# Merging the map chains of two batches, and queueing mixing earlier, in a gated cross-attention and stream-mixing kernel

## The chip, the cores and the metric

The kernel runs on one core of a Trainium2 chip. The metric is the device time of one execution in microseconds. The kernel before takes 1831.41 us (median of 3 runs, 1829.26 to 1835.13). The execution that the profiler recorded took 1828.05 us, of which its span, from the first recorded instruction to the last, is 1825.9 us.

The engines are named as in the profile: PE (TensorE, matmul), PEld (its weight loads), DVE (VectorE), ACT (ScalarE), POOL (GpSimd) and SP (SyncE, which issues every transfer here). Each runs its own list of instructions in order, and they wait for each other through semaphores.

## The reference

The input x has 8 batches of 512 rows and 2048 columns. There are two residual stages, each on a layer-normed x.

```python
x = x + tanh(g_xattn) * xattn(layernorm(x), ctx, mask, Wq..bo)
x = x + tanh(g_ffn)   * ffn(layernorm(x), W_res, W_pre, W_post, ...)

# ffn: every row is a token of 4 streams of 512
x_norm = x * rsqrt(mean(x*x) + eps)
H_res  = sinkhorn(x_norm @ W_res.T + base, 50 iterations, tau=0.1)   # 4x4
H_pre, H_post = softmax(x_norm @ W_pre.T + ..), softmax(x_norm @ W_post.T + ..)
H_res  = (1-g)*I + g*H_res
y      = (sum_n H_pre[n] * x[n]) @ W_branch
out[i] = sum_j H_res[i,j] * x[j] + H_post[i] * y
```

The first stage cuts the 2048 columns into patches of 128 and runs attention with 8 heads inside each patch. The second stage needs a whole row of the first stage's result before it can begin: the layer norm and the 24 logits of a token are sums over all 2048 columns. From the logits it makes the token's maps (a 4 x 4 matrix by Sinkhorn's iteration, and two softmaxes of 4), and then mixes the four streams with them.

## The kernel before, in words

**The main loop.** A batch has 16 patches, so there are 128 patches in order, counted by t. For each t the function `act` emits the pieces of work that the letters of ORDER name: scores and their maxima (`smax`, three patches ahead), exponentials (`expo`), attention times values (`attv`), output projection (`outp`), the projections of a later block of four patches (`proj`, `stack`, `vproj`), statistics of a later batch (`stats`), and steps of mixing (`mixstep`). The result x1 of the first stage goes to DRAM (x1s).

**The chain of maps.** When the last block of a batch has been projected (`outp` of block n-1, at t = 16(b+1) + 3), `rawmap` gathers the batch's sums and `ffn` emits its maps. A batch has 512 tokens, which lie as 4 groups on 128 partitions, so a 4 x 4 matrix per token makes tiles of 128 x 64 (E, L, W) and 128 x 16 (sm, uv). After a prologue of norms, logits and softmaxes come 49 sweeps of six DVE instructions each, L844 to L854: multiply, row sum, reciprocal, multiply, column sum, reciprocal. Each needs the result of the one before it. Every ten sweeps the scale factors are folded back with a logarithm and an exponential on ACT (L858, L840). L873 writes the finished map Et. This dependent series is called the chain of that batch.

CHAINS says which batches form one chain. `ffn` takes a list of batches and makes its tiles 4 groups wide for each; NTM, the width for which tiles are reserved, is four times the longest entry of CHAINS. A chain is emitted when its last batch is complete.

**Mixing.** There are two forms. `mixv` (L909 to L951) works on 128 tokens, called a chunk, mostly on DVE: it loads four streams, makes the weighted sum xpre with ACT and POOL, runs the branch matmul, and makes each of the four outputs with L939 (ACT), L943/L944 (ACT, POOL), L946 and L949 (DVE). The main loop takes its steps from a queue, mixq: an entry may begin at t + LAGS[b], where t is the patch at which the chain was emitted, and then 3.25 steps are taken per patch. A chunk has 13 steps.

`mixp` (L953 to L1005) works on a chunk mostly on PE. Its first half loads the rows (xc), makes xpp with four matmuls (L967), transposes it (L974) and runs the branch matmuls (L905 to L907, with plb made on DVE at L902). Its second half multiplies with two matrices QD and HD (L1000, L1001), which POOL builds (L988, L990). HD is built from HR, which is the batch's Et written to DRAM (L885) and read back in another layout (L887). PD, for the first half, is built from rec, which takes the same way (L796, L798) but is ready early in the chain. PE_MIX says which chunks are mixed in this way: chunk 3 of batch 4, all of batches 5 and 6, and chunks 1 to 3 of batch 7. They are kept in tailq and run after the last patch, in this order. They are written (4,3), (5,0) and so on below. The last pieces are those of batch 7's remaining chunk, a `mixv`.

**The order on each engine** isn't written by hand. A scheduler places the instructions of each engine by readiness in its own timing model and by priority, and the engine then runs the list in that order. The pieces have priority 0, and the chain has -1000, so a chain instruction that is ready goes first. A tile pool with n buffers makes the n-plus-first user wait for the first one's readers.

The lines that the change touches:

```python
LAGS = (30,) * 8                                                      # L53
CHAINS = ((0,), (1,), (2,), (3,), (4,), (5,), (6,), (7,))             # L81
PE_MIX = ((), (), (), (), (3,), (0, 1, 2, 3), (0, 1, 2, 3), (1, 2, 3))# L79
NTM = 4 * max(len(c) for c in CHAINS)                                 # L713
for grp in CHAINS:                                                    # L1112
    if grp[-1] == bb_ - B + 8:
        ...
        res = at("chain", ffn, grp)
        for q, maps in zip(grp, res):
            mixq.append((t + LAGS[bb_], mix(q, maps)))
            for c_ in PE_MIX[q - B]:
                tailq.append(mixp(q, c_, maps))
```

Of the kernel before, what the change touches and what calls it, by code (L numbers as in the profile page):

```python
# [49 lines left out]
PRI = dict(load=0, smax=0, expo=0, attv=0, outp=0, proj=0, stack=0, vproj=0, stats=0, mix=0, chain=-1000, raw=0)  # L50
EARLY = 4
LATE = 3000
LAGS = (30,) * 8  # L53
NV = 2
MIXN = 2
MIXP = (3.25,)*4
# [21 lines left out]
BUF_XP = 16  # L78
PE_MIX = ((), (), (), (), (3,), (0, 1, 2, 3), (0, 1, 2, 3), (1, 2, 3))  # L79
SPLITS = (1, 1, 1, 1, 1, 1, 1, 1)  # L80
CHAINS = ((0,), (1,), (2,), (3,), (4,), (5,), (6,), (7,))  # L81
BUF_SK = 2
PE_IN = ((), (), (), (), (), (), (), ())
HDP = 'xtp'
# [15 lines left out]
def gated_xattn_mhc_kernel(  # L100
# [611 lines left out]

    NTM = 4 * max(len(c) for c in CHAINS)  # L713

# [176 lines left out]
    def mix(b, maps):  # L891
        E, cst, pre, prc, post, rec, HR = maps
        for c in range(4):
            if c in PE_IN[b - B]:
                yield from mixp(b, c, maps, True)
            elif c not in PE_MIX[b - B]:
                yield from mixv(b, c, maps)
# [149 lines left out]
    def act(c, t):  # L1047
# [54 lines left out]
        elif c == "O":  # L1102
# [3 lines left out]
            if n >= 1 and p == 3:  # L1106
                at("outp", run, og_[0])
                bb_, kk_ = divmod(n - 1, NBLK)
                if kk_ == NBLK - 1:
                    at("raw", rawmap, bb_)  # L1110
                    p0 = tc.cur_priority
                    for grp in CHAINS:  # L1112
                        if grp[-1] == bb_ - B + 8:
                            grp = [q + B - 8 for q in grp if q + B - 8 >= 0]
# [4 lines that stand above are left out]
# [77 lines left out]
```

## Time and profile before

| | |
|---|---|
| median of 3 runs | 1831.41 us (1829.26 to 1835.13) |
| profiled execution | 1828.05 us, span 1825.9 us |
| granted PE clock, mean | 0.932 |
| PE busy | 1547.1 us, 85% |
| DVE busy | 1382.3 us, 76% |
| ACT busy | 1069.4 us, 59% |
| POOL busy | 602.8 us, 33% |
| 49 sweeps of 8 chains on DVE (L844 to L854, records added up) | 606.8 us in 2312 instructions |
| the chain of batch 0, first copy to Et | about 300 to 508 us |
| of batch 5 | about 1320 to 1610 us |
| of batch 6 | about 1515 to 1703 us |
| of batch 7 | 1642 to 1769 us |
| exponential of the last patch (L597) | between 1610 and 1620 us; the tail then runs to 1826 us |

How to read the rows below. A row of busy time by stage gives the stretch, its length, then the busy time of PE, PEld, DVE, ACT and POOL with the number of instructions, the granted clock of PE (1.00 is full), the share of the DMA engines and GB/s. If it is asked for one source line, it has only the engine of that line. A row of the time order gives start, duration, engine, line, operation, output and inputs, shape, and in brackets how long the engine had been idle before it and what ended that. Records of neighbouring DVE instructions can overlap: what an instruction costs its neighbours is the distance between starts.

### The profile page before, as it was taken

The numbers are of one execution on the slowest core, as the hardware profiler recorded it, in microseconds if no ns is written. First come the engines' busy times: TensorE is split into PE (matmuls) and PEld (weight loads), VectorE is DVE, ScalarE is ACT, GpSimd is POOL, SyncE is SP. The second block draws the span as 40 slices with busy tenths as digits, with TensorE's granted clock in tenths as the row PEclk, the third lists the DMA queues.
The fourth block names the chain that finished last, engine by engine and source line by source line (L and its number), as shares of the span: only waits on it lengthen the run. The fifth ranks groups of instructions, "written<-read, shape, count | busy, mean of one in ns | idle before, by whom it ended". The sixth has DMA issues, their size and how long they took to land.

```text
span 1825.9 us, 32268 instructions
## 1 busy us (share of the span) xinstructions
PE 1547.1 (85%) x10517; PEld 901.0 (49%) x10517; DVE 1382.3 (76%) x4201; ACT 1069.4 (59%) x2030; POOL 602.8 (33%) x511
## 2 busy tenths in 40 slices
PE   3998999989889888889878888799888889768887
PEld 2554555555555554545544445455455555543333
DVE  7434345877888778888888879889898998998761
ACT  2386466646555656558565475566665566755454
POOL 0512222322232243342444333444334442321121
PEclk7999999999999988999988999899999999989999
DMA  6478696467646855568555784468755565523443
GB/s 214 139 209 256 208 258 194 140 174 232 180 134 200 254 169 165 151 192 269 162 154 164 214 251 144 139 196 259 215 154 165 148 189 147 172 93 119 144 157 117
DMA packets 353237, 330.60 MB, mean 181 GB/s; under 512 B 53351, under 2 KB 251303, under 8 KB 353070
## 3 DMA queue, kind: packets, MB, share of 16 engines
q1 hardware_dynamic: 353070, 328.55, 60.6%
q8 instruction: 83, 1.36, 0.3%
q14 instruction: 84, 0.69, 0.1%
HBM read 226.71 MB, written 101.16 MB: 180 GB/s over the span
## 4 chain that ended last, share of the span: by engine, by line
PE 37%; DVE 23%; DMA 18%; issue 9%; ACT 9%; POOL 4%; SPq 1%; ACTq 0%; POOLq 0%; DVEq 0%
PE vp L559 5%; DVE w L946 4%; DMA xs<-in_x_dram 4%; PE qk L518 3%; PE qk L519 3%; DMA out_dram<-w 3%; PE qk L520 3%; DMA x<-x1s 2%; PE mx L1000 2%; DMA x1s<-xt 2%; PE lgx L448 2%; DVE mx L571 2%; PE op L667 2%; DVE W L844 2%; PE mx L1001 2%
## 5 line engine op out<-in xcount | busy, mean ns | idle before, releaser
L559 PE MATMUL vp<-Wv,ct 128*128 128x256 f32 x1024 | 272.4, 418 | 16.7 <-DMA ct<-in_cx_dram 15.1
L500 POOL TENSOR_SCALAR xn<-xt,ln_r,nb 128x512 f32<-128x512 f32 x128 | 105.5, 826 | 501.2 <-DMA xt<-in_x_dram 385.7
L559 PEld LDWEIGHTS vp<-Wv,ct 128*128 128x128 f32 x1024 | 207.4, 210 | 68.0 <-issue 18.6
L518 PE MATMUL qk<-xh,WqkH 128*128 128x512 f16 x512 | 199.2, 390 | 29.4 <-ACT xh L505 16.3
L946 DVE SCALAR_TENSOR_TENSOR w<-x,Et,w 128x512 f32<-128x512 f32 x180 | 180.0, 1001 | 49.6 <-POOL w L944 34.0
L519 PE MATMUL qk<-xl,WqkH 128*128 128x512 f16 x512 | 197.9, 387 | 4.3 <-POOL xl L507 4.0
L520 PE MATMUL qk<-xh,WqkL 128*128 128x512 f16 x512 | 197.6, 386 | 0.0
L571 DVE TENSOR_REDUCE mx<-smax 128x8 f32<-128x1024 f32 x128 | 154.9, 1210 | 41.7 <-PE smax L569 41.3
L507 POOL TENSOR_TENSOR xl<-xn,xh 128x512 f16<-128x512 f32 x128 | 156.3, 1228 | 76.0 <-ACT xh L505 70.4
L597 ACT ACTIVATE e<-sT,ebi,esc 128x1024 f32<-128x1024 f32 x128 | 153.4, 1198 | 18.0 <-PE sT L595 17.9
L523 DVE SCALAR_TENSOR_TENSOR ev<-qk,bqs,ev 128x512 f16<-128x512 f32 x128 | 94.5, 739 | 77.5 <-ACT ev L522 76.1
L667 PE MATMUL op<-gh,WoH 128*128 128x512 f32 x256 | 120.9, 474 | 35.3 <-DVE ev L523 31.1
L944 POOL TENSOR_TENSOR w<-w,pj 128x512 f32<-128x512 f32 x60 | 80.1, 1334 | 213.1 <-ACT w L939 113.7
L505 ACT CAST xh<-xn 128x512 f16<-128x512 f32 x128 | 78.3, 612 | 103.7 <-POOL xn L500 102.9
L522 ACT ACTIVATE ev<-qk,bqs 128x512 f16<-128x512 f32 x128 | 86.9, 679 | 85.0 <-PE qk L520 78.7
L673 ACT ACTIVATE junk<-xt,nmean 128x512 bf16<-128x512 f32 x128 | 91.6, 716 | 73.9 <-DVE xt L671 41.3
L850 DVE TENSOR_TENSOR W<-E,uv 128x64 f32<-128x64 f32 x392 | 119.4, 307 | 5.4
L844 DVE TENSOR_TENSOR W<-E,uv 128x64 f32<-128x64 f32 x352 | 117.1, 335 | 4.8
L612 PE MATMUL u<-e,onesb 128*32 128x256 f32 x1024 | 102.7, 403 | 10.5 <-DVE mq L573 3.8
L668 PE MATMUL op<-gl,WoH 128*128 128x512 f32 x256 | 107.1, 418 | 0.0
L669 PE MATMUL op<-gh,WoL 128*128 128x512 f32 x256 | 106.6, 417 | 0.0
L632 POOL TENSOR_TENSOR o<-o,mb 128x1024 f32<-128x1024 f32 x32 | 75.6, 2364 | 93.2 <-ACT o L627 85.9
(287 smaller groups left out, 3504.6 us busy)
## 6 DMA issues: line engine op xcount, KB each, us to landing
xt<-in_x_dram SPq DMA_DIRECT2D x128, 256.0 KB
ct<-in_cx_dram SPq DMA_DIRECT2D x128, 256.0 KB
xTt<-in_xT_dram SPq DMA_DIRECT2D x128, 256.0 KB
qd<-ev SPq DMA_DIRECT2D x128, 256.0 KB
x1s<-xt SPq DMA_DIRECT2D x128, 256.0 KB
xs<-in_x_dram SPq DMA_DIRECT2D x112, 256.0 KB
QS<-qd SPq DMA_DIRECT2D x192, 128.0 KB
KS<-qd SPq DMA_DIRECT2D x192, 128.0 KB
```

The source lines that it names most:

```text
L507: G.tensor_tensor(l, xn, h, ALU.subtract)
L518: T.matmul(ps, WqkH[:, c, ms], hs[c], start=(c == 0), stop=False)
L519: T.matmul(ps, WqkH[:, c, ms], ls[c], start=False, stop=False)
L520: T.matmul(ps, WqkL[:, c, ms], hs[c], start=False, stop=(c == 3))
L559: T.matmul(ps[:, h, :], ct[:, c, :], Wv[:, c, :], start=(c == 0), stop=(c == 3))
L571: V.tensor_reduce(mx, sc, AX.X, ALU.max)
L597: A.activation(e32, sc, AF.Exp, bias=ebi[:, t : t + 1], scale=esc[:, t : t + 1])
L667: T.matmul(ps, WoH[:, e, cs], gh[:, e], start=(e == 0), stop=False)
L668: T.matmul(ps, WoH[:, e, cs], gl[:, e], start=False, stop=False)
L844: V.tensor_tensor(W4[:, h], E4[:, h], vb[:, h], ALU.mult)
L850: V.tensor_tensor(W4[:, h], E4[:, h], ub[:, h], ALU.mult)
L946: V.scalar_tensor_tensor(w, x1[j], E[:, n, 4 * j + i : 4 * j + i + 1], w, ALU.mult, ALU.add)
```

## The change

Two constants change. Batches 1 and 2 share a chain, as do 3 and 4, and 5 and 6; batches 0 and 7 keep their own. A chain of two batches is emitted at the patch at which its second batch was emitted before (t = 51, 83 and 115), and its tiles are 8 groups wide: 128 x 128 for E, L and W, 128 x 32 for sm and uv. As NTM is now 8, the tiles of batches 0 and 7 are the first half of such tiles. LAGS is looked up by the batch that completes the chain, so every entry but batch 0's is now 18. Both batches of a pair are queued for mixing at the same patch: 69 for batches 1 and 2 (65 and 81 before), and 101 for batches 3 and 4 (97 and 113 before). The order of tailq is the same.

```diff
-LAGS = (30,) * 8
+LAGS = (30, 18, 18, 18, 18, 18, 18, 18)
-CHAINS = ((0,), (1,), (2,), (3,), (4,), (5,), (6,), (7,))
+CHAINS = ((0,), (1, 2), (3, 4), (5, 6), (7,))
```

## The prediction

> **What bounds the kernel now.** I read the page's busy shares first, then busy time by stage, then the time order of DVE, PE and POOL after the last patch. The stages are cut where a batch's chain begins (its first copy, L710 and L724), so each but the last is the time of 16 patches.
>
> ```profile
> span 1825.9 us, 32268 instructions
> PE 1547.1 (85%) x10517; PEld 901.0 (49%) x10517; DVE 1382.3 (76%) x4201; ACT 1069.4 (59%) x2030; POOL 602.8 (33%) x511
> ...
> 297.00:471.00 174.00, 157.21 (x1174) 96.18 (x1168) 129.19 (x407) 103.44 (x208) 51.82 (x46) 0.96 0.63 183
> 883.00:1105.00 222.00, 183.00 (x1283) 109.14 (x1282) 184.76 (x554) 132.78 (x259) 86.41 (x69) 0.92 0.64 188
> 1323.00:1514.00 191.00, 165.60 (x1191) 102.12 (x1190) 175.03 (x502) 117.04 (x214) 84.11 (x68) 0.93 0.57 167
> 1642.00:1826.00 184.00, 156.86 (x484) 56.47 (x482) 114.56 (x530) 89.38 (x157) 28.71 (x32) 0.99 0.40 136
> ```
>
> The columns are PE, PEld, DVE, ACT, POOL, granted clock, DMA. Sixteen patches with one chain and no mixing take 174 us (10.9 a patch); with mixing 222 and, once the statistics are done, 191. TensorE is the busiest engine throughout, at 90% without mixing and 82% with it, and DVE comes close (92% in the third row). So DVE relief can pay there, but only where PE waits for it. The last 184 us have no attention left: PE works through the PE chunks.
>
> ```profile
> 1645.72 1.12 PE L1000 MATMUL mx<-ys,QD 128*128 128x512 f32 x2 [0.68 <-ACT ys L985]
> 1660.43 0.38 PE L907 MATMUL yp<-WbH,plb 128*128 128x512 f16 x1
> 1661.48 1.12 PE L1000 MATMUL mx<-ys,QD 128*128 128x512 f32 x2 [0.68 <-ACT ys L985]
> 1675.92 1.10 PE L1000 MATMUL mx<-ys,QD 128*128 128x512 f32 x2 [0.77 <-ACT ys L985]
> ...
> 1703.14 0.25 DVE L873 TENSOR_TENSOR Et<-E,eye 128x64 f32<-128x64 f32 x1
> ...
> 1708.82 1.05 POOL L990 TENSOR_TENSOR HD<-blk,HR 128x512 f32<-128x512 f32 x1 [8.70 <-DMA HR<-hd]
> ```
>
> One PE chunk takes 14.4 us (1661.48 to 1675.92), with waits under 1 us: PE sets the end. The last two lines are the hinge. Chain 6 delivers its maps (Et) at 1703.4, they go out to DRAM and back as HR, and HD, which the second half of chunk (6,0) needs, is ready at 1709.9: 6.5 us after Et. PE reaches that half at about 1719. Chain 5 had ended at about 1610, so chunks (5,0) to (5,3) waited for nothing.
>
> **The change, part 1: fewer, wider DVE instructions.** The instruction lists of the two builds have 4077 and 3105 rows of DVE: three chains of some 324 instructions go. What is one worth? Two stretches of DVE in time order, first two chains side by side, then one alone:
>
> ```profile
> 1661.50 0.26 DVE L852 TENSOR_REDUCE sm<-W 128x16 f32<-128x64 f32 x1
> 1661.68 0.21 DVE L846 TENSOR_REDUCE sm<-W 128x16 f32<-128x64 f32 x1
> 1661.80 0.24 DVE L854 RECIPROCAL uv<-sm 128x16 f32<-128x16 f32 x1
> 1661.96 0.21 DVE L848 RECIPROCAL uv<-sm 128x16 f32<-128x16 f32 x1
> ...
> 1720.48 0.25 DVE L854 RECIPROCAL uv<-sm 128x16 f32<-128x16 f32 x1
> 1720.77 0.22 DVE L844 TENSOR_TENSOR W<-E,uv 128x64 f32<-128x64 f32 x1
> 1721.03 0.22 DVE L846 TENSOR_REDUCE sm<-W 128x16 f32<-128x64 f32 x1
> ```
>
> Alternating, instructions start 0.143 us apart on average (58 from 1661.5 to 1669.8); alone, each waits for the one before and they start 0.275 apart. So merging two chains removes mostly latency that overlapped anyway. The Trainium skill's page "VectorE: DVE Perf Modes", section "The DRAIN you can't avoid", says that after each DVE operation the pipe has to empty[...]; its text lets operations that aren't held start earlier. By the strict rule 972 removed instructions are worth 972 x 0.275 = 267 us of DVE; by the row, standing beside other work, 972 x 0.143 = 139. I take the row.
>
> The width costs: no row has 128 columns. L755 on 96 columns takes 0.25 against 0.22 on 64, so 64 more cost some 0.065; the reduce L571 (1024 columns, 1.21 us) against L852 (64, 0.26) gives 1 ns a column, the same 0.065; a reciprocal of 8 takes 0.20 (L768), of 16 0.25, so 16 more cost 0.10. Mean over the six instructions of a sweep 0.077; three chains of some 300: 69 us. DVE's net relief is 139 - 69 = 70 us by the row, 198 by the rule.
>
> How much reaches the end? In the list of waits by stage, PE's rows that name DVE add up to 15.6, 15.5, 26.0 and 9.7 us in the four mixed stages from 665 to 1514, about 1 us in each of their 64 patches; and PE's clock falls after gaps (0.92 against 0.96 on 183 us of busy PE: another 0.5 us a patch). That is the ceiling: 1.5 us in each patch without a chain. In the changed DVE list such patches are those between smax 42 and 57, 79 and 89, 111 and 120: 34 patches, so at most 51 us. For the floor, a count of expo (L597, one a patch) where one chain is live beside mixing, and where two are:
>
> ```profile
> 735.00:905.00 170.00, 14.80 (x13) 0.95 0.67 197
> 905.00:985.00 80.00, 7.96 (x7) 0.91 0.55 162
> 985.00:1135.00 150.00, 13.21 (x11) 0.90 0.65 195
> 1340.00:1430.00 90.00, 8.16 (x7) 0.91 0.61 174
> ```
>
> One chain (first and third): 320 us for 24 patches, 13.3 each; two (second and fourth): 170 us for 14, 12.1. A second chain costs nothing that can be seen (each count may be off by one), which speaks for little relief. I take 0.6 us x 34 = 20 us gained, between 0 and 51.
>
> **Part 2: the queueing of mixing.** Batch 1 is queued at patch 51 + 18 = 69 instead of 65, and the rest follow: mixing ends near patch 129, not 125. But the maps of (1,2) come only at smax 79 and those of (3,4) at smax 111, so in the list mixing stands still in between (52 mix instructions from smax 72 to 79) and then runs at 5.5 to 6 per patch instead of 3.25. The work is the same 247 instructions; ACT, 59% busy, has room. Moved, not removed: 0, with 10 us either way. The wide chains while mixing runs are as dense as two narrow ones: 0.
>
> **Part 3: chain (5,6) ends late.** It is emitted where chain 6 was (patch 115). Where chain 7 starts (T0, 1641.9 in the trace), the changed list has it at 20 of 49 sweeps done, and its Et (L873) stands 362 DVE instructions later, alternating with chain 7. Their time: the first 90 as now, 19 us (1641.9 to 1660.6), plus 2.5 for width; the other 272 at 0.143 = 39 and 136 wide ones at 0.077 = 10.5; two round trips to ACT 1.5; two plb of PE chunks 2.5. Sum T0 + 75. Bounds: 68 with no waits, 84 with waits for phb like those now (2.1 and 2.3 us each).
>
> Until then PE has, in list order: (4,3) and the first half of (5,0), done at T0 + 19 as now (1660.8); two L1000 of (5,0), 2 us; the first halves of (5,1) and (5,2), 9 us each (4 xpp at 1 us, transposes and ACT waits 2, yp 3); one xpp of (5,3). That is T0 + 40. Then L1001 waits for HD: SP issues two hd and two HR (0.4 us more than now), HD at T0 + 75 + 7 = T0 + 82. **PE stands 42 us**, 34 to 51. Queued behind on PE is everything: 165 - 21 = 144 us of chunk work. On SP, behind L885, stand three of the four xc loads of (5,3); on POOL, behind that HD, the next QD and HD; they land within the 8 us of second halves that PE has ready. Restart at low clock: now 0.50 in the 5 us window after the 7.5 us gap at 1619, so 2 us for cold matmuls, less about 1 that the full run of second halves saves in ACT waits. Tail: +43. Chain 7's own end, about 50 us after Et at 0.275 a piece, comes before (7,1).
>
> **The sum** is made against the profiled execution: 1828.05 us (span 1825.9 and 2.15 around it), + 43 - 20 + 0 = 1851. The median of the runs, 1831.41, is 3.4 above it; I say 1852.
>
> **Rivals.** (A) As above: +8 to +43, 1839 to 1874. (B) Faster: the relief is what the rule says, 198 us of DVE, and PE gets the ceiling, 51 us, or more where the chain is absent in the mixed stages; from 44 us of gain on (1.3 us in each of 34 patches) it beats the tail. With 57 us: 1814 to 1822. For it speaks DVE at 92% in the third stage row; against it, that two chains side by side cost no more than one. (C) The two cancel: gain 38 to 49, within 0.3%. (D) No relief: the bursts of mixing put DVE, ACT (0.8 us per L939) and the one-buffer pj and POOL adds in a queue of their own, and the wide chain, at 0.35 us per step instead of 0.14, delays ev: gain 0 or a loss of 10, 1871 to 1884. (E) That the change doesn't do what it says: a lag of 18 isn't reached, since Et comes 25 patches after emission; this is in the list already and so in A.
>
> **Chances.** A 0.57, B 0.17, C 0.09, D 0.17. Slower 0.74, same 0.09, faster 0.17, with 0.3% (5.5 us) taken as what can be told from no change. The range 1816 to 1879 leaves out the lower half of B and the upper part of D.
>
> **What would show it.** PE idle of 34 to 51 us in one piece some 40 us after the last patch, ended by HD L990, itself by HR; DVE down to about 3200 records; L850 on 128 columns near 0.29 us; the start of chain 7 at 1610 to 1635 instead of 1642. If that start lies before 1598, or PE shows no such wait because POOL or SP got HR earlier, the forecast is wrong on the fast side; if it lies after 1642, on the slow side.

## The result, and the profile after

The changed kernel takes 1909.36 us (median of 4 runs, 1907.91 to 1911.76), the kernel before 1832.09 in the same session (1829.26 to 1835.13). The ratio is 1.043, interval 1.040 to 1.046: some 77 us slower. The forecast was 1852 us, range 1816 to 1879. The sign was right, and the size was not.

The page after, its span and the engines' busy time:

```profile
span 1910.0 us, 31196 instructions
PE 1560.9 (82%) x10455; PEld 911.0 (48%) x10517; DVE 1276.9 (67%) x3166; ACT 1062.3 (56%) x1976; POOL 598.8 (31%) x511
```

DVE lost 1035 records and 105 us of busy time, and no other engine's busy time moved by more than 14 us. DVE did get the relief that the change aims at. The span still grew by 84.1 us, so most of it is waiting and not work.

Busy time by stage, the stages cut where they were cut before. Columns: the stretch, its length, then PE, PEld, DVE, ACT, POOL, granted clock, share of DMA, GB/s:

```profile
297.00:471.00 174.00, 156.15 (x1172) 95.81 (x1180) 130.93 (x410) 102.51 (x208) 51.96 (x45) 0.96 0.64 186
870.00:1105.00 235.00, 182.50 (x1238) 107.98 (x1246) 152.04 (x301) 130.87 (x240) 85.70 (x69) 0.90 0.60 178
1325.00:1535.00 210.00, 169.55 (x1198) 106.65 (x1199) 149.96 (x294) 121.16 (x207) 83.77 (x68) 0.89 0.51 148
1680.00:1910.00 230.00, 165.29 (x503) 60.00 (x501) 132.84 (x565) 92.42 (x163) 29.43 (x34) 0.90 0.34 112
```

The first stage is as before. In the second and third DVE's share fell, from 83% to 65% and from 92% to 71%, yet they take longer than the stages that held the same patches (222 and 191 us). PE's share fell with it. So neither engine's busy time is the limit there.

A finer cut shows where this happens. Each patch has one exponential (L597 on ACT), and its start times were read out of both traces:

| stretch, by the start of a patch's L597 | before, us | after, us | difference |
|---|---|---|---|
| start to patch 51 | 635.5 | 635.9 | +0.4 |
| 51 to 71 | 278.5 | 259.3 | -19.2 |
| 71 to 75 | 51.1 | 79.8 | **+28.7** |
| 75 to 79 | 56.7 | 41.9 | -14.8 |
| 79 to 103 | 318.0 | 329.9 | +11.9 |
| 103 to 107 | 39.7 | 81.5 | **+41.8** |
| 107 to 111 | 56.7 | 34.0 | -22.7 |
| 111 to 127 | 177.8 | 183.2 | +5.4 |
| 127 to the end | 211.9 | 264.5 | **+52.6** |

The differences add up to 84.1 us. By patch 71 the changed kernel is 19 us ahead; from patch 51 on it has run 14 groups of mixing there and the kernel before 20. Two groups of four patches then lose 70 us and get 37 back right after, a net loss of 33, and the tail is longer. Inside the two groups it is one patch each: 39.9 us for patch 74 (it took 10.1) and 43.2 for patch 106 (4.1). This is ACT in time order through patch 74:

```profile
943.62 1.52 ACT L939 ACTIVATE w<-x,sm,Et 128x512 f32<-128x512 f32 x2
945.05 0.71 ACT L943 ACTIVATE pj<-x,Et 128x512 f32<-128x512 f32 x1
...
950.68 0.81 ACT L939 ACTIVATE w<-x,sm,Et 128x512 f32<-128x512 f32 x1 [2.22 <-DMA out_dram<-w]
952.87 0.72 ACT L943 ACTIVATE pj<-x,Et 128x512 f32<-128x512 f32 x1 [1.38 <-POOL w L944]
953.50 0.80 ACT L939 ACTIVATE w<-x,sm,Et 128x512 f32<-128x512 f32 x1
957.36 0.81 ACT L920 ACTIVATE xpre<-x,prc,pre 128x512 f32<-128x512 f32 x1 [3.05 <-DMA x<-x1s]
...
960.37 0.81 ACT L939 ACTIVATE w<-x,sm,Et 128x512 f32<-128x512 f32 x1 [1.35 <-DVE w L949]
...
966.04 0.81 ACT L939 ACTIVATE w<-x,sm,Et 128x512 f32<-128x512 f32 x1
...
972.70 0.72 ACT L673 ACTIVATE junk<-xt,nmean 128x512 bf16<-128x512 f32 x1 [2.39 <-PE y L906]
```

The first L939 starts 0.4 us after the maps of (1,2) (Et, L873, 943.21). ACT then needs 29 us for six groups of mixing and the beginning of the next chunk. It is busy for 12.8 of them; the rest is waits for stores and loads and for POOL, DVE and PE. Of attention only one eviction (L522) stands between them. L673, which squares a finished result of attention, stands in the list behind them, and starts at 972.7. The last 2.4 us of that are a wait for the mixing's branch (L906): L673 writes its scratch output to the one buffer that the branch uses too. What that holds up, from the waits of the same stretch (SP's, and then PE's; us in total, times, the longest):

```profile
SPq L233 <- ACT junk L673: 10.1, 1, 10.1
```

```profile
PE xpT L931 <- POOL xpre L925: 4.6, 1, 4.6
PE op L667 <- DVE ev L523: 2.7, 1, 2.7
```

L233 loads the next x of attention into a buffer that L673 still has to read. SP issues every transfer here, so for 10 us nothing else went out either (its list has nothing between 963.3 and 973.5). PE, for its part, had the mixing's branch (L931) ahead of the next attention in its list and waited for POOL's sum. In this patch PE was busy 26.9 of 40 us, and in the 40 us before it 31.6. How much of the loss each of these waits makes was not separated. The granted clock (the first number after POOL's) fell from 0.91 to 0.83:

```profile
895.00:935.00 40.00, 31.58 (x239) 20.35 (x239) 28.57 (x78) 18.64 (x34) 12.52 (x11) 0.91 0.45 122
935.00:975.00 40.00, 26.87 (x123) 15.35 (x124) 26.71 (x49) 16.91 (x28) 9.45 (x7) 0.83 0.41 133
```

The reason for the six groups is in the instruction list. The changed DVE list has 52 mix instructions (L946, L949) done at smax 79, where Et of (1,2) stands, and 72 at smax 80: twenty within one patch. The same happens for (3,4), with 156 at smax 111 and 176 at smax 112. Anywhere else in it a patch has at most nine. (The list's smax runs some five patches ahead of the expo count.) Mixing of (1,2) was queued from patch 69 on, at 3.25 steps a patch, and for six patches had no maps to run with. All of what was due then stands right behind Et.

The tail, in time order of PE, DVE and POOL:

```profile
1683.52 0.23 DVE L724 COPY raw<-raw 128x136 f32<-128x136 f32 x1
...
1731.41 1.02 PE L967 MATMUL xpp<-xc,PD 128*32 128x512 f32 x2 [2.65 <-issue]
1758.96 0.37 DVE L873 TENSOR_TENSOR Et<-E,eye 128x128 f32<-128x128 f32 x1
1764.48 1.04 POOL L990 TENSOR_TENSOR HD<-blk,HR 128x512 f32<-128x512 f32 x1 [43.78 <-DMA HR<-hd]
1765.58 3.78 PE L1001 MATMUL mx<-xc,HD 128*128 128x512 f32 x4 [33.15 <-POOL HD L990]
```

This is the hinge of the forecast, and it moved as forecast: T0 (L724 of chain 7) 1683.5, Et at T0 + 75.4, HD at T0 + 82.0, and PE stands 33 us in one piece. From T0 to the end it is 226.5 us against 184.0.

### The profile page after: what moved, and what is told of

Same layout as the page of the kernel before. It is cut to its first block, busy times and chain, and to the rows that moved or that the text cites. A ratio compares the mean times of both kernels' runs of the same rounds, so it can differ in the third digit from the quotient of the medians.

```text
span 1910.0 us, 31196 instructions
## 1 busy us (share of the span) xinstructions
PE 1560.9 (82%) x10455; PEld 911.0 (48%) x10517; DVE 1276.9 (67%) x3166; ACT 1062.3 (56%) x1976; POOL 598.8 (31%) x511
## 4 chain that ended last, share of the span: by engine, by line
PE 22%; DVE 16%; DMA 12%; issue 6%; ACT 5%; POOL 3%; SPq 1%; another core or an unknown queue 0%; ACTq 0%; POOLq 0%; DVEq 0%
PE vp L559 4%; DVE w L946 3%; DMA x<-x1s 2%; DMA out_dram<-w 2%; PE mx L1000 2%; PE mx L1001 2%; DVE mx L571 2%; DMA xt<-in_x_dram 1%; DMA x1s<-xt 1%; DVE W L850 1%; DMA ct<-in_cx_dram 1%; DVE W L844 1%; PE op L667 1%; DVE w L949 1%; DVE ev L523 1%
## 5 line engine op out<-in xcount | busy, mean ns | idle before, releaser
L559 PE MATMUL vp<-Wv,ct 128*128 128x256 f32 x1024 | 279.1, 426 | 30.0 <-DMA ct<-in_cx_dram 21.8
L559 PEld LDWEIGHTS vp<-Wv,ct 128*128 128x128 f32 x1024 | 213.0, 215 | 82.1 <-issue 14.2
L946 DVE SCALAR_TENSOR_TENSOR w<-x,Et,w 128x512 f32<-128x512 f32 x180 | 174.4, 970 | 59.0 <-POOL w L944 33.2
L519 PE MATMUL qk<-xl,WqkH 128*128 128x512 f16 x512 | 199.2, 389 | 15.5 <-POOL xl L507 15.5
L520 PE MATMUL qk<-xh,WqkL 128*128 128x512 f16 x512 | 198.5, 388 | 0.0
L597 ACT ACTIVATE e<-sT,ebi,esc 128x1024 f32<-128x1024 f32 x128 | 153.5, 1199 | 16.0 <-PE sT L595 15.9
L522 ACT ACTIVATE ev<-qk,bqs 128x512 f16<-128x512 f32 x128 | 87.0, 680 | 105.3 <-PE qk L520 100.5
L673 ACT ACTIVATE junk<-xt,nmean 128x512 bf16<-128x512 f32 x128 | 91.7, 716 | 76.1 <-PE y L906 40.8
L671 DVE TENSOR_TENSOR xt<-op,xt 128x512 f32<-128x512 f32 x128 | 87.3, 682 | 40.1 <-remote 22.5
L569 PE MATMUL smax<-KS,QS 97*128 97x128 f16 x1024 | 88.1, 226 | 30.9 <-ACT e L597 8.7
L668 PE MATMUL op<-gl,WoH 128*128 128x512 f32 x256 | 105.5, 412 | 0.0
L481 ACT ACTIVATE xs<-xs,nmean 128x512 f32<-128x512 f32 x112 | 79.9, 715 | 44.6 <-DMA xs<-in_x_dram 33.8
```

The lines of the kernel that those rows point to most:

```text
L519: T.matmul(ps, WqkH[:, c, ms], ls[c], start=False, stop=False)
L520: T.matmul(ps, WqkL[:, c, ms], hs[c], start=False, stop=(c == 3))
L559: T.matmul(ps[:, h, :], ct[:, c, :], Wv[:, c, :], start=(c == 0), stop=(c == 3))
L597: A.activation(e32, sc, AF.Exp, bias=ebi[:, t : t + 1], scale=esc[:, t : t + 1])
L668: T.matmul(ps, WoH[:, e, cs], gl[:, e], start=False, stop=False)
L946: V.scalar_tensor_tensor(w, x1[j], E[:, n, 4 * j + i : 4 * j + i + 1], w, ALU.mult, ALU.add)
```

## The experiments

The table has all runs. "Last patch" is the start of the last L597, "tail" from there to the end of the profiled span, "left" the groups of mixing (L939) after it, "longest patch" one L597 to the next, from patch 33 on. The ratio is to the kernel before, measured on the same chip. All columns behind it are from one profiled execution, and the executions of one kernel differ by 4 to 27 us.

| run | median, us | ratio (95%) | last patch | tail | left | longest patch (groups in it) |
|---|---|---|---|---|---|---|
| before | 1831 to 1835 | 1 | 1614.0 | 211.9 | 4 | 31.1 (2) |
| the change | 1909.4 | 1.043 (1.040 to 1.046) | 1645.5 | 264.5 | 6 | 43.2 (6), 39.9 (6) |
| pair56 | 1868.8 | 1.017 (1.013 to 1.021) | 1611.3 | 255.4 | 4 | 30.1 (2) |
| pairs1234 | 1886.1 | 1.027 (1.023 to 1.032) | 1658.2 | 222.0 | 6 | 47.2 (6), 41.2 (6) |
| pairs_lag30 | 1875.3 | 1.021 (1.015 to 1.026) | 1578.2 | 294.5 | 18 | 32.1 (2) |
| lag18all | 1845.2 | 1.006 (1.004 to 1.008) | 1635.9 | 210.2 | 4 | 34.0 (5) |
| defer | 1864.9 | 1.018 (1.013 to 1.022) | 1590.0 | 276.1 | 18 | 30.0 (2) |
| pairs1234_lag30 | 1857.1 | 1.015 (1.010 to 1.021) | 1599.9 | 251.4 | 18 | 31.8 (2) |
| pairs_lag24 | 1884.2 | 1.029 (1.024 to 1.033) | 1607.8 | 275.2 | 11 | 32.2 (4) |
| split2 | 1907.5 | 1.042 (1.038 to 1.047) | 1632.7 | 262.1 | 6 | 36.1 (6) |
| lag30_fast | 1912.9 | 1.042 (1.037 to 1.046) | 1662.8 | 250.4 | 6 | 44.0 (4) |
| after_w3 | 1926.7 | 1.050 (1.047 to 1.053) | 1663.3 | 261.5 | 5 | 48.5 (7), 35.7 (7) |
| lag24all | 1858.4 | 1.013 (1.008 to 1.018) | 1634.8 | 216.5 | 4 | 35.5 (3) |
| pairs1234_l30_fast | 1838.3 | 1.003 (1.001 to 1.005) | 1591.0 | 243.9 | 14 | 33.0 (2) |
| lag30_r425 | 1866.8 | 1.019 (1.015 to 1.023) | 1599.7 | 274.9 | 14 | 33.3 (2) |
| p1234_l25_r425 | 1853.8 | 1.012 (1.010 to 1.014) | 1632.9 | 223.4 | 6 | 32.8 (4) |
| before_r425 | 1841.8 | 1.005 (1.001 to 1.008) | 1624.0 | 214.8 | 4 | 30 or less |

### The tail alone: pair56

```diff
 (the kernel before)
-CHAINS = ((0,), (1,), (2,), (3,), (4,), (5,), (6,), (7,))
+CHAINS = ((0,), (1,), (2,), (3,), (4,), (5, 6), (7,))
```

> The kernel before with one edit: only the chains of batches 5 and 6 run as one (lags stay 30; 1, 2, 3, 4 stay single). Two theories share out the 77 us that the whole change cost. Theory S (stand and burst): the pairs (1,2) and (3,4), whose mixing stands in the engines' lists ahead of their maps, cost some 31 to 38 us by the last patch, and the late pair (5,6) costs 43 to 46 us in the tail. Then this kernel loses the tail alone: PE waits 30 to 45 us in one piece for HD of (6,0), chain 7 starts within 6 us of where it starts before, time 1872 to 1880. Theory T (the tail only looks long because everything before it is late, and cold clock carries over): this kernel is within 15 us of the time before.

The last patch comes 2.7 us earlier than before and the tail is 43.5 us longer in the profiled execution. By the medians the whole kernel is slower by 24 to 39 us. The waits of its tail:

```profile
POOL HD L990 <- DMA HR<-hd: 42.0, 1, 42.0
PEld mx L1001 <- POOL HD L990: 31.9, 2, 31.7
PE mx L1001 <- POOL HD L990: 29.9, 1, 29.9
```

The late pair costs 35 us (1868.8 against 1834.1) with no other edit in the kernel, by the wait that the forecast names. Theory T falls, and the time is 3 us below what theory S gave.

### The patches alone: pairs1234

```diff
 (the changed kernel)
-CHAINS = ((0,), (1, 2), (3, 4), (5, 6), (7,))
+CHAINS = ((0,), (1, 2), (3, 4), (5,), (6,), (7,))
```

> The changed kernel with 5 and 6 single again; (1,2), (3,4) and the lag of 18 stay. Theory S: the tail is that of the kernel before (184 us after the start of chain 7), the loss by the last patch stays, 31 to 38 us, time 1862 to 1872. The forecast's step (pairs gain 20 us, the queueing of mixing costs 0) would give 1811. A third view, that the loss by the last patch comes from the chain of (5,6) running in the mixed stage beside the end of mixing, would give 1820 to 1835.

It was slower than either theory said, 52 us and not 31 to 38. The same two patches are there (74 and 106, 41.2 and 47.2 us, six groups in each), and PE has no long wait in the tail (222.0 us). A difference to the changed kernel's patches is that chain 5 starts at patch 99 here, beside mixing and chain (3,4). In the changed kernel its work waits for 6 and runs in the tail. So the two losses, 35 and 52, don't add up to 77: with 5 and 6 merged the last patch comes 13 us earlier (1645.5 against 1658.2). That it is chain 5 which makes these 13 us was not tested.

### Mixing queued later: pairs_lag30 and pairs_lag24

```diff
 (the changed kernel)
-LAGS = (30, 18, 18, 18, 18, 18, 18, 18)
+LAGS = (30,) * 8                            # pairs_lag30
+LAGS = (30, 24, 24, 24, 24, 24, 24, 24)     # pairs_lag24
```

> The changed kernel with all lags at 30: the three pairs stay, mixing is queued at about patch 81 and 113, when the maps of its pair are there (their last operations stand at patch 80 and 114 of the list). Theory S: no mixing stands ahead of its maps, so the loss of 29 us around patch 75 and of 42 us around patch 107 goes; patches without mixing run as in the part of the trace with chain alone; what mixing is left falls beside PE's wait in the tail. Tail still 43 to 46 us longer; time 1865 to 1885, some 25 to 45 below the changed kernel. The rival, that the wide chain itself delays evictions (an instruction of 0.36 us instead of 0.14), has nothing to do with the queueing: time 1900 to 1915.

> The changed kernel with lags 24 in place of 18 (30 for batch 0): mixing of (1,2) is queued at patch 75 and not 69, that of (3,4) at 107 and not 101 or so, against maps at 79 and 111; about 16 to 20 mix instructions stand in the list where the change has 52 and, by then, its backlog. If the loss follows the amount of mixing that stands ahead of its maps: about a third to a half of the 34 us between lags 18 and 30 remains, time 1883 to 1896. If any stand at all costs the same (the engines' lists only have to meet once): 1900 to 1912. If only the free stretch without mixing counts: 1875 to 1885.

34 us come back with the lag of 30, as theory S has it, and 25 with 24. The 1884.2 us of lag 24 fit two of the three views written for it: that part of the loss remains (1883 to 1896), and that only the stretch without mixing counts (1875 to 1885). In the list with lag 24 there are 52 mix instructions at smax 79 and 52 at smax 80, and then at most ten in a patch. The two patches of 40 us are gone. ACT in time order behind the maps of (1,2), lag 24:

```profile
948.66 1.52 ACT L939 ACTIVATE w<-x,sm,Et 128x512 f32<-128x512 f32 x2 [2.69 <-DVE Et L873]
950.09 0.71 ACT L943 ACTIVATE pj<-x,Et 128x512 f32<-128x512 f32 x1
950.70 0.71 ACT L673 ACTIVATE junk<-xt,nmean 128x512 bf16<-128x512 f32 x1
951.31 0.19 ACT L673 ACTIVATION_READ_ACCUMULATOR junk<-xt,nmean 128x1 f32 x1
...
952.13 1.18 ACT L597 ACTIVATE e<-sT,ebi,esc 128x1024 f32<-128x1024 f32 x1
...
960.68 0.81 ACT L939 ACTIVATE w<-x,sm,Et 128x512 f32<-128x512 f32 x1 [0.32 <-DMA out_dram<-w]
```

Here L673 comes 2.0 us and the next L597 3.5 us behind the start of the first groups, with two groups before them. In the changed kernel L673 came after six, 29 us behind.

My expectation for lag 24 was wrong in its list: I wrote that 16 to 20 instructions would still stand there. There are none. With lag 30, 18 groups of mixing are left for the tail and with 24 it is 11, against 6. So some of what the patches gain is moved, not saved. The next two runs measure that.

### Is it moved work: defer and pairs1234_lag30

```diff
 (the kernel before: single chains, mixing held to patches 81 and 113)
-LAGS = (30,) * 8
+LAGS = (30, 46, 30, 46, 30, 30, 30, 30)     # defer
 (pairs1234)
-LAGS = (30, 18, 18, 18, 18, 18, 18, 18)
+LAGS = (30,) * 8                            # pairs1234_lag30
```

> The kernel before with single chains, mixing of batches 1 and 2 held until patch 81, of 3 and 4 until patch 113 (lags 30, 46, 30, 46, 30 ...), as the three pairs with lag 30 have it: no mixing stands ahead of its maps. With the pairs at lag 30 the last patch started 36 us earlier than before, and 14 more groups of mixing (L939) ran after it. Theory M (moved mixing): those 36 us are the moved mixing, 14 times some 2.5 us, and not fewer DVE instructions. Then this kernel too has its last patch 25 to 40 us earlier, with no chain merged, and 1800 to 1828, as the tail pays back some of it. Theory R (relief): the 36 us come from the 972 removed instructions. Then the last patch starts within 8 us of the kernel before, and the time is 1828 to 1845.

> Pairs (1,2) and (3,4), lag 30, batches 5 and 6 single. Theory of this study: no stand of mixing ahead of maps, no late pair in the tail; what is left is the relief and the moved mixing. Last patch 25 to 50 us earlier than in the kernel before, tail longer by 5 to 30 us, time 1800 to 1825, better than the kernel before. If merging itself costs (an instruction of 0.36 us ahead of evictions), the time is above that of the single chains held back in the same way, by 10 us or more.

The last patch of `defer` comes 24 us earlier, with no chain merged, so most of the 36 us was moved mixing (theory M, though 1 us short of its span). But I had the tail wrong, and with it the time (1864.9, not 1800 to 1828): it is 64 us longer, for 14 more groups. I had thought that DVE, ACT and POOL were nearly free there. PE waits for HD again in that tail, though no chain was merged:

```profile
  DMA HR<-hd: 25.0, 4
...
  PE mx L1001: 14.4, 2
```

These are rows of HD's line (L990): what POOL waited for, and what PE waited for it. Chain 6 delivers its Et at 1776.1, against 1703.1 in the kernel before. So with mixing held back the last chains come late too, though none is wide.

`pairs1234_lag30` has the same queue and 690 fewer DVE records. It was to be faster than the kernel before (1800 to 1825) and is 26 us slower. Against `defer` it is 8 us faster (1857.1 against 1864.9), but their runs overlap (1852 to 1872 and 1857 to 1869). That is what is left of the relief with mixing queued alike, and it isn't told apart from nothing.

### Width or place: split2

```diff
 (the changed kernel)
-SPLITS = (1, 1, 1, 1, 1, 1, 1, 1)
+SPLITS = (1, 1, 2, 1, 2, 1, 2, 1)
```

> The changed kernel, its merged chains run as two interleaved halves (SPLITS 2 for the pairs): DVE has the 972 narrow instructions back, the chains stay in their merged places and the lag is 18. Maps come one or two patches earlier in the list (smax 78 and 110). If the width of an instruction (0.36 us, each waiting for the one before) made evictions and maps late: the time falls by 20 us or more, to 1860 to 1890. If it is place and queueing, not width: 1900 to 1920.

1907.5 us with 4060 DVE records, against 1909.4 with 3166. 894 more DVE instructions, half as wide and interleaved, make no difference that can be told, though DVE is busy 32 us longer (1308.8 against 1276.9). The patch with six groups is there (36.1 us). So trading width against count does nothing while the place of the chains and the queueing stay. The run changes the two together; neither was varied alone.

### Does the burst or the wait for maps cost: lag30_fast, after_w3

```diff
 (pairs_lag30)
-MIXP = (3.25,)*4
+MIXP = (5.5,)*4          # lag30_fast
 (the changed kernel)
-BUF_W = 2
+BUF_W = 3                # after_w3
```

> The three pairs with lag 30, and mixing let through at 5.5 instructions a patch and not 3.25 once it is queued. In the list no mixing stands ahead of its maps (52 mix instructions done at patch 80, maps of (1,2) at 80; 156 at 112, maps of (3,4) at 112), but it runs as dense after them as in the changed kernel, and 215 and not 192 of 247 are done by the last patch. Theory S (what costs is mixing that stands ahead of its maps): within 12 us of the pairs with lag 30 at the slow rate (1875), so 1863 to 1887; the patches get about 15 us longer and the tail as much shorter. Theory B (what costs is the burst after the maps): 1893 to 1915.

> The changed kernel with three buffers for the tile w and not two. In its trace ACT waits 13.9 us in 9 places for a w to be stored before the next L939. Theory B (the burst after the maps costs, and the w buffers pace it): 10 to 25 us faster, 1885 to 1900. Theory S (the loss is made while mixing stands, before any w is written): 1903 to 1914.

Theory S in the form in which I had written it falls. In `lag30_fast` no mixing is due before its maps, and yet it takes 1912.9 us. The loss is made in other places: patches 91 to 99 lose 37 us against the kernel before with 13 groups in eight patches (8 before), and patches 119 to 127 lose 41 with 16 (6 before). Against `pairs_lag30` it has 12 more groups before the last patch and gets there 84.6 us later, 7.1 us for each of them; the tail gives 44 back. So mixing that stands ahead of its maps isn't needed for a loss of this size. What the lossy places have in common is density: a backlog that falls due at once, or a higher rate. That is read from where the loss falls, and it is no rule for every rate: 4.25, below, costs 8 us or gains 19, depending on the kernel.

A third buffer for w made the changed kernel 17 us slower, where I expected it to be faster or to do nothing. Some 11 us of the 17 are lost in patches 71 to 75 (90.9 us against 79.8); patch 106 is shorter than before (35.7 us against 43.2), and the rest is spread. ACT in time order in patch 74:

```profile
958.94 1.52 ACT L939 ACTIVATE w<-x,sm,Et 128x512 f32<-128x512 f32 x2 [3.79 <-DVE Et L873]
960.36 0.70 ACT L943 ACTIVATE pj<-x,Et 128x512 f32<-128x512 f32 x1
960.98 0.80 ACT L939 ACTIVATE w<-x,sm,Et 128x512 f32<-128x512 f32 x1
...
976.81 0.81 ACT L939 ACTIVATE w<-x,sm,Et 128x512 f32<-128x512 f32 x1 [0.88 <-DMA out_dram<-w]
```

With two buffers the third L939 stood 5.5 us behind the first two; with three it follows them after 0.5. Seven groups and not six run in this patch, and it takes 48.5 us. The list shows the same: 23 mix instructions between smax 79 and 80, not 20. This fits with the short buffer having held the burst down.

### The queueing alone: lag18all, lag24all

```diff
 (the kernel before)
-LAGS = (30,) * 8
+LAGS = (18,) * 8         # lag18all
+LAGS = (24,) * 8         # lag24all
```

> The kernel before with all lags at 18, single chains. Mixing of batch 0 is queued before its maps are there, so its instructions stand in the lists ahead of them, with no pair anywhere. Theory S: each such stand costs 10 to 20 us where it occurs; later batches have a backlog and so stand less. Time 1842 to 1875. The rival (the lag is harmless, the pair is the cause): 1826 to 1838.

> The kernel before with all lags at 24: single chains, mixing of each batch queued right where its maps stand in the list (52 done at patch 61, maps at 61; 104 at 78, maps at 78), against 18 where it stands 4 to 8 patches ahead (11 us slower) and 30 where it follows some 15 patches behind. Theory S: no stand, time 1826 to 1838, about the kernel before. If mixing that follows its maps without any distance is late in time though not in the list: 1838 to 1848.

Lag 18 with single chains costs 0.4 to 0.8%, in the expected range. It has up to five groups in a patch (34.0 us), runs 62 us behind the kernel before at patch 107, and gets 40 of them back by patch 127, because its mixing ends some ten patches earlier. A lag of 24 was to be harmless, and cost 0.8 to 1.8%. It is 39 us behind the kernel before at patch 115: 16 of them are lost in patches 43 to 51, where it runs eight groups of mixing and the kernel before none, and the rest a few us at a time. Why mixing close behind its maps costs more than mixing ahead of them was not settled. That a shorter lag costs something even with single chains is measured. But a lag of 18 isn't the loss by itself: it costs 10 us with single chains (1845.2) and leaves 52 where (1,2) and (3,4) are merged (`pairs1234`).

### The rate, and both causes out

```diff
-MIXP = (3.25,)*4
+MIXP = (4.25,)*4         # in pairs1234_lag30: pairs1234_l30_fast
                          # in pairs_lag30: lag30_r425; in the kernel before: before_r425
 (pairs1234_l30_fast)
-LAGS = (30,) * 8
+LAGS = (30, 25, 25, 25, 25, 30, 30, 30)     # p1234_l25_r425
```

> Pairs (1,2) and (3,4), lag 30, 5 and 6 single, mixing at 4.25 instructions a patch and not 3.25: 202 and not about 190 of 247 mix instructions done by the last patch, the rest in the tail. If a group of mixing costs about the same in the patches as in the tail (2.5 us): 1850 to 1864, as at 3.25. If it costs more in the tail (39 us longer for 14 groups, 2.8 each, and chains late behind it): 1835 to 1850. Below 1826 it would beat the kernel before; that would need the relief to show, which it has not so far.

> The three pairs, lag 30, mixing at 4.25 instructions a patch (between 3.25, which gave 1875, and 5.5, which gave 1913). Same as pairs (1,2) and (3,4) at 4.25 (1838), but for 5 and 6 merged. If the late pair (5,6) costs its own 35 to 45 us whatever stands before it: 1872 to 1884. If three pairs are worse than the sum at any rate above 3.25 (a full DVE and mixing crowd each other): 1890 to 1905.

> Pairs (1,2) and (3,4), 5 and 6 single, lags 25 for batches 1 to 4, 4.25 mix instructions a patch: queued at patch 76 and 108, so that no backlog is due when the maps come (52 mix instructions at patch 80, maps at 80; 156 at 112, maps at 112), and 226 of 247 are done by the last patch. With both causes out (the queued backlog released in one patch; the late pair) this should be about the kernel before: 1826 to 1842. If merging has a loss of its own that lag 30 hid by moving mixing into the tail: 1845 to 1860. A patch of 35 us or more with six L939 in it would say that the backlog is still there.

> The kernel before with mixing at 4.25 instructions a patch, nothing else. It says how much of the 19 us between pairs (1,2), (3,4) at 3.25 (1857) and at 4.25 (1838) is the rate alone. Here mixing has no backlog to work off, so the rate only bunches it: 1830 to 1845; a gain of more than 6 us (below 1826) would say that the rate itself pays, with no chain merged.

`pairs1234_l30_fast` is the best version with merged chains: 1838.3 us, 0.1 to 0.5% slower than the kernel before. It has neither the block of twenty nor the late pair. The rate isn't a gain by itself (`before_r425` is 8 us slower); here it takes four groups out of the crowded tail (14 left, not 18). With 5 and 6 merged as well (`lag30_r425`) it is 28.5 us more, 1866.8 against 1838.3. That is less than the 35 to 45 expected for this difference, though the time itself is 5 us below the range given for it. In the profiled executions the tail is 31 us longer (274.9 against 243.9) and the last patch 8.7 us later.

`p1234_l25_r425` was to be about the kernel before and is 20 us slower. Its list has no block (at most seven mix instructions in each of the patches right behind a pair's maps), and no patch is above 32.8 us, though five groups still meet in patch 77 (31.5 us). The time lies in the span written for a loss of merging that lag 30 had hidden in the tail (1845 to 1860). With lag 25 it puts 74 groups in the patches where lag 30 put 66, and reaches the last patch 41.9 us later: 5.2 us for each of these eight. The maps of a pair come late (smax 80 and 112, where a single chain's come at 62 and 96 for batches 1 and 3), so the same mixing has fewer patches left. It is either dense there or it is left for the tail, and both cost.

## Why the prediction was wrong

**The step that failed is part 2, the queueing of mixing put at 0.** It said of mixing: "The work is the same 247 instructions; ACT, 59% busy, has room. Moved, not removed: 0, with 10 us either way." With part 1's gain the sum was -20 at the start of chain 7, and it was +41.6 (1683.5 against 1641.9). These 62 us are the whole error of the forecast (1911.8 against 1851 in the profiled execution). What had been costed at 0 cost 61 us if the 19 us gained by patch 71 are relief, and 42 if they are not; the next paragraph says why they are not. I had read the list, and had in hand that mixing stands still until smax 79 and then runs "at 5.5 to 6 per patch". That is a mean over ten patches, and it hid that 20 of 55 stand within one patch. An engine that is 59% busy on average has no room at a place where its list holds six groups in a row and attention stands behind them. The two patches cost 70 us and gave 37 back. Lag 24, which takes the block of twenty out of the list, gave 25 us of the 77, and lag 30 34; `after_w3`, which makes the block larger, cost 17 more. The other side of the step is that the mixing couldn't be moved for nothing either: merged maps come late, so with lag 30 the mixing runs late, and that costs 26 us with (1,2) and (3,4) merged and 34 with no chain merged at all (`defer`).

**Part 1, the relief, had the instruction right and its worth wrong.** The wide instructions cost what was estimated. Chain (3,4) in time order on DVE:

```profile
1396.32 0.29 DVE L844 TENSOR_TENSOR W<-E,uv 128x128 f32<-128x128 f32 x1
1396.65 0.29 DVE L846 TENSOR_REDUCE sm<-W 128x32 f32<-128x128 f32 x1
1396.97 0.35 DVE L848 RECIPROCAL uv<-sm 128x32 f32<-128x32 f32 x1
1397.36 0.29 DVE L850 TENSOR_TENSOR W<-E,uv 128x128 f32<-128x128 f32 x1
1397.68 0.38 DVE L852 TENSOR_REDUCE sm<-W 128x32 f32<-128x128 f32 x1
1398.09 0.35 DVE L854 RECIPROCAL uv<-sm 128x32 f32<-128x32 f32 x1
```

The starts lie 0.32 to 0.41 us apart, 0.35 on average (0.275 + 0.077 had been worked out). But the relief reached no end. By the records of L844 to L854, the changed kernel runs no chain in patches 40 to 53, 75 to 86 and 107 to 118. The last two stretches follow the two long patches and hold what comes back after them. The first can be read alone, from the start of patch 40 to that of patch 54, with four groups of mixing in both kernels (before, then after):

```profile
511.40:687.70 176.30, 154.55 (x1116) 95.11 (x1114) 139.72 (x398) 103.35 (x202) 60.60 (x51) 0.94 0.65 190
508.50:683.30 174.80, 154.64 (x1134) 96.44 (x1141) 87.85 (x167) 101.48 (x195) 58.48 (x50) 0.94 0.67 194
```

DVE is busy 52 us less, PE as before, and 14 patches take 1.5 us less: 0.1 a patch, where 0.6 had been taken and 1.5 was the ceiling. The 19.2 us by patch 71 come later, and that they are close to the 20 forecast for the whole run is luck: 14.4 of them fall in patches 54 to 71, where the wide chain runs, and ten groups of mixing instead of sixteen. `defer`, with no chain merged, gains 15.2 us there with twelve groups, and `split2`, with 894 more DVE records than the change, 19.1 with ten. So what was gained there goes with mixing that comes later. The strict rule of the Trainium skill ("VectorE: DVE Perf Modes", section "The DRAIN you can't avoid", by which the next operation waits until the pipe is empty), with the 198 us of net relief estimated from it, would have made the change faster. In this case's rows the operations of two alternating chains start 0.143 us apart and last 0.21 us and more, so they don't wait in that way.

**Part 3, the tail, held almost number for number.** Et at T0 + 75 (75.4), HD at T0 + 82 (82.0), from T0 to the end +43 (226.5 - 184.0 = 42.5). One term was off: PE got through its chunks by T0 + 49, not T0 + 40 (it was busy for 35.8 of the 49 us), so that it stood 33 us and not 42. That changed nothing at the end, because the end is set by HD and by what is queued behind it: 144.5 us from HD on (226.5 - 82.0), where 144 of chunk work and 1 for the restart had been taken. The single-edit run (`pair56`) shows the same wait of 30 us, and a cost of 24 to 39 us.

**The rivals.** D, no relief and bursts of mixing, came nearest: no relief, and the right queue, but with a loss of 10 us at most, where 42 were lost by the start of chain 7. Its other half, that a wide instruction delays the evictions, was not borne out (`split2`). B, the faster end, had nothing to show at any lag or rate. The sentence on what would show the forecast wrong on the slow side, chain 7 starting after 1642, is what happened.

**What stays open.** In one order the edits do account for the 77 us, each kernel taken against the kernel before on its chip: splitting (5,6) takes the loss from 77 to 52, queueing at lag 30 from 52 to 26, and `defer` loses 34 with its mixing queued in the same way and nothing merged. Of the 61 us lost between patch 71 and the start of chain 7, though, only the net 33 of the two places are located; 12 in patches 79 to 103, and 15 from patch 111 on, aren't explained by a run. `lag24all` is slower than both its neighbours and no run says why. And the costs don't add up in another order: 35 us for the pair (5,6) and 52 for the rest, alone, against 77 together; the pair (5,6) costs 18, 23 and 28.5 us where (1,2) and (3,4) are merged too (`pairs_lag30`, the change and `lag30_r425`, each against the same kernel with 5 and 6 single).

## What to carry to other kernels

When queued work has to wait for a result, look at how much of it is due when the result comes, and count it in the instruction list per step and not as a mean over ten: what is due at once can stand ahead of everything else in each in-order list. Making a dependent series shorter by joining two of them makes the first one's result as late as the second's, and the price is set by who waits for the first. Relief of a busy engine counts only where something waits for it: 52 us less on DVE moved 14 patches by 1.5 us. An idle share of an engine is worth something only where its list lets other work in between, and a stretch at the end that looks free may be setting the end of the last chains.

## What the runs showed of the hardware

PE ran slower after most waits of more than 2 us. In patch 74 the same f32 matmul (L668) took 0.40 us at 950.19 and 0.63 at 951.02, just after a wait of 2.7 us for ev, and its kind stayed at 0.63 to the end of that group (955.2). Taking the matmuls of L519, L520, L668, L669, L906 and L907 that start 0.7 to 2.5 us after a stretch without matmuls, in all 17 traces: most of them lasted over 0.5 us, and not 0.4, after 27 of 292 such stretches of 0.5 to 1 us, after 45 of 65 of 2 to 3 us, and after all 32 of 3.5 us or more. While PE stood for HD (1731 to 1766) the granted clock was 0.52, and in the 24 us after that 0.92. So a wait can cost more than its length: from T0 to the end PE runs 484 matmuls in the kernel before and in the changed one, and was busy 157.0 us in the one and 162.5 in the other.

A group of mixing has no fixed price. Going from `pairs_lag30` to `lag30_fast` each further group before the last patch cost 7.1 us there, and from `pairs1234_l30_fast` to `p1234_l25_r425` 5.2. In the tail the 14 groups that `defer` moved there cost 4.6 each (64.2/14), with a wait for HD among it.
